# The first attention of a four-layer block: another order of its tiles, outputs kept by channel and divided with the help of DMAs and GpSimd, row maxima turned by VectorE

## The chip, the cores and the metric

The kernel runs on one core of one Trainium2 chip. The metric is the device time of one execution in microseconds (us); less is better. Each engine of the core works through a queue of its own: TensorE (PE; PEld is its loading of weights), VectorE (DVE), ScalarE (ACT), GpSimd (POOL) and SyncE (SP), which here does nothing but issue DMAs.

## What is computed

Four layers follow each other, each with a layer norm before it and a residual sum after it: an attention with 32 heads of 16 channels, a feed-forward layer with routed low-rank experts (FFN), an attention with 32 query heads of 128 channels, and the FFN again. The input has 1024 tokens of 512 channels, all in float32. Only the first attention is touched, and the projection after it:

```python
x = x + _L0_attn_a_ref(_layernorm(x, axis=-1), wq, wk, wv, wo)
# in it, with rotary embedding on xq and xk:
scores = jnp.einsum('bqhd,bkhd->bhqk', xq, xk) * scale
scores = jnp.where(causal[None, None], scores, NEG_INF)
probs = jax.nn.softmax(scores.astype(jnp.float32), axis=-1)
out = jnp.einsum('bhqk,bkhd->bqhd', probs, xv).reshape(B, T, C)
return out @ wo.T
```

## The kernel before

**Tiling.** The 32 heads are worked in 8 chunks (`NCA`) of 4 heads (`HC`). A head's 16 channels are padded to 32 partitions (`PADA`), so that the four heads of a chunk lie in the four quarters of `qT` and `kT` (128 partitions, chunk, 1024 tokens), and four score matmuls with 32 rows each can run beside each other in TensorE. Tokens come in 8 tiles of 128 (`NT`), queries also in two halves of 512 (`QC`; `qc` or `half` 0 is the low half).

**Two passes of scores.** The softmax needs the maximum of each query's row. So scores are made twice. The *row pass* (`row_scores`, L304) has queries on partitions; VectorE takes from it the negative maxima (`maxima`, L319) into `neg`. `with_maxima` (L341) turns `neg` so that queries lie along the free axis, and writes it into row 16 (`DA`) of every head in `qT`, where `kT` holds ones. The *column pass* (`col_scores`, L355) of the same chunk then has keys on partitions and yields scores with the maximum already subtracted; ScalarE takes the exponential (`exponentials`, L371), and `product` (L384) multiplies with the values. `v_p` has a 17th column of ones, so the products bring the sums of each row along, as row 16 of each head. A causal mask is added by one bf16 matmul per head on blocks on the diagonal (L380).

**Order.** `step(rc, cc, n)` (L440) does the n-th piece of the row pass of chunk `rc` and of the column pass of chunk `cc = rc - 1` together. It has two halves; in each, two heads make column scores and the other two make row scores, so that all four quarters of TensorE are in use. Then come maxima, exponentials, what is due from the list `later`, and half of the product of the step before last. The pieces of a chunk are listed by hand in `by_rows` and `by_cols` (L269 to L272): ten steps a chunk, of which two have 256 columns and the others 512; blocks on the diagonal occur in six of them. The row pass of chunk 0 runs in the prologue among the projections of q, k and v. The column pass begins with the low half; its maxima are written during the row pass's chunk, and those of the high half after step 0 of the column pass, which first uses them in step 3.

**Outputs.** When a half is complete, ScalarE copies it from PSUM (L407). One step later `normalize` (L410) transposes it on TensorE to tokens on partitions (L414), ScalarE copies it (L417), VectorE inverts the sums (L419), GpSimd multiplies in four pieces (L421) into `o`. After the last chunk `gather` (L1013) transposes `o` back to channels on partitions, tile by tile, and `out_projection` (L1019) multiplies with the output weights and adds to the residual: two tiles in `tail`, six among the first FFN.

**Queues and buffers.** All DMAs of this stage stand on SP's queue; the weights of the projection and the FFN are loaded on GpSimd's in the middle of it (`midway`). Score tiles share seven PSUM buffers (`ps_s`), outputs have one (`ps_o`). Waits between engines are set by the framework from what instructions read and write. An engine's order mostly follows the program, but the framework may lay an instruction later when it expects its inputs later.

Of the kernel before, what the change touches and what calls it, by code (L numbers as in the profile page):

```python
# [16 lines left out]
P = 128  # L17
T = 1024
# [46 lines left out]
class Block:  # L65
# [174 lines left out]
    def attend_a(self, ctx_pool, pt, work, ps_s, ps_o, qT, kT, v_p, project_qk, project_v, midway, tail):  # L240
        nc, tc = self.nc, self.tc
        HC = P // PADA
        with ExitStack() as ctx:
            cp = ctx.enter_context(tc.tile_pool(name="a_c", bufs=1))
            qk = ctx.enter_context(tc.tile_pool(name="a_qk", bufs=2))
            o_sb = []
# [22 lines left out]
            by_rows = [[(3, 0)], [(2, 0), (0, 0)], [(1, 0)], [(4, 0)], [(5, 0)], [(6, 0)], [(7, 0)]]  # L269
            by_rows += [[(7, 1)], [(6, 1), (4, 1)], [(5, 1)]]  # L270
            by_cols = [[(0, 0)], [(0, 1), (0, 3)], [(0, 2)], [(1, 0)], [(1, 1)], [(1, 2)], [(1, 3)]]
            by_cols += [[(1, 4)], [(1, 5), (1, 7)], [(1, 6)]]  # L272
            NP = len(by_rows)
# [21 lines left out]
            def row_pieces(n):  # L295
                return list(placed(by_rows[n], lambda i, kc: min(QC, (i + 1) * P - kc * QC)))

            def col_pieces(n):
                return list(placed(by_cols[n], lambda qc, b: min(QC, (qc + 1) * QC - b * P)))

            def on_diagonal(qc, b):
                return b * P >= qc * QC

            def row_scores(c, n, heads, made):  # L304

                for j in heads:
                    made[j] = ps_s.tile([P, QC], F32, tag="s", name=f"s{c}_{n}_{j}")
                for i, kc, at, end in row_pieces(n):
                    for j in heads:
                        nc.tensor.matmul(  # L310
                            made[j][:, at:end],
                            lhsT=qT[rows_of(j), c, i * P : (i + 1) * P],
                            rhs=kT[rows_of(j), c, kc * QC : kc * QC + end - at],
                            start=True,
                            stop=True,
                        )
                        yield

            def maxima(c, n, heads, made):  # L319

                for j in heads:
                    for i, kc, at, end in row_pieces(n):
# [18 lines left out]
            def with_maxima(c, half):  # L341

                rows = HC * NT // 2
                ps = ps_s.tile([P, QC], F32, tag="s", name=f"tp_m{c}{half}")[:rows, :P]
                nc.tensor.transpose(ps, neg(c, half).rearrange("p h i -> p (h i)"), self.ident)
                t = qk.tile([P, P], F32, tag="negT", name=f"negT{c}_{half}")[:rows, :]
                nc.scalar.copy(t, ps)
                for j in range(HC):
                    row = j * PADA + DA
                    nc.sync.dma_start(  # L350
                        qT[row : row + 1, c, half * QC : (half + 1) * QC].rearrange("o (i t) -> o i t", t=P),
                        t[j * NT // 2 : (j + 1) * NT // 2, :],
                    )

            def col_scores(c, n, heads, made):  # L355

                pieces = col_pieces(n)
                for j in heads:
                    made[j] = ps_s.tile([P, QC], F32, tag="s", name=f"sT{c}_{n}_{j}")
                for x, (qc, b, at, end) in enumerate(pieces):  # L360
                    for j in heads:
                        nc.tensor.matmul(  # L362
                            made[j][:, at:end],
                            lhsT=kT[rows_of(j), c, b * P : (b + 1) * P],
                            rhs=qT[rows_of(j), c, (qc + 1) * QC - (end - at) : (qc + 1) * QC],
                            start=x == 0,
                            stop=x == len(pieces) - 1 and not on_diagonal(qc, b),
                        )
                        yield

            def exponentials(n, heads, made, p):  # L371
                pieces = col_pieces(n)
                end = pieces[-1][-1]

                if on_diagonal(*pieces[0][:2]):
                    step = pieces[-1][2] // P or 1
                    mask = maskT.unsqueeze(1).to_broadcast([P, len(pieces), P])
                    for j in heads:
                        to = made[j].rearrange("p (a k) -> p a k", k=P)[:, : (len(pieces) - 1) * step + 1 : step, :]
                        nc.tensor.matmul(to, lhsT=identb, rhs=mask, start=False, stop=True)  # L380
                for j in heads:
                    nc.scalar.activation(p[:, j, :end], made[j][:, :end], AF.Exp)  # L382

            def product(c, n, p):  # L384

                first, last = n in (0, 3), n in (2, NP - 1)
                pieces = col_pieces(n)
                qc, middle = pieces[0][0], pieces[-1][-1] // 2
                if first:
                    outs[c, qc] = ps_o.tile([P, QC], F32, tag="o", name=f"oT{c}_{qc}")  # L390
                o = outs[c, qc]
                for lo, hi in ((0, middle), (middle, 2 * middle)):
                    for _, b, at, end in pieces:
                        x0, x1 = max(lo, at), min(hi, end)
                        for j in range(HC if x0 < x1 else 0):
                            nc.tensor.matmul(  # L396
                                o[rows_of(j), QC - end + x0 : QC - end + x1],
                                lhsT=v_cols(b, c * HC + j),
                                rhs=p[:, j, x0:x1],
                                start=first and x0 == 0,  # L400
                                stop=last and x1 == 2 * middle,
                            )
                    yield
                if not last:
                    return
                oT = work.tile([P, QC], F32, tag="w", name=f"oTs{c}_{qc}")
                nc.scalar.copy(oT, o)  # L407
                later.append(lambda: normalize(c, qc, oT))

            def normalize(c, qc, oT):  # L410
                if not o_sb:
                    o = ctx_pool.tile([P, NT, C], F32, tag="o", name="o")
                    o_sb.extend(o[:, i] for i in range(NT))
                ps = self.transpose4(ps_s, [oT[:, i * P : (i + 1) * P] for i in range(4)], f"o{c}{qc}", tag="s")  # L414
                pv = ps.rearrange("p a (h d) -> p a h d", d=PADA)
                os = qk.tile([P, 4, HC, DA + 1], F32, tag="os", name=f"os{c}_{qc}")
                nc.scalar.copy(os, pv[:, :, :, : DA + 1])  # L417
                rs = qk.tile([P, 4, HC], F32, tag="rs", name=f"rsa{c}_{qc}")
                nc.vector.reciprocal(rs, os[:, :, :, DA])  # L419
                for a in range(4):  # L420
                    nc.gpsimd.tensor_tensor(  # L421
                        o_sb[qc * 4 + a][:, c * HC * DA : (c + 1) * HC * DA].rearrange("p (h d) -> p h d", d=DA),
                        os[:, a, :, :DA],
                        rs[:, a, :].unsqueeze(2).to_broadcast([P, HC, DA]),
                        ALU.mult,
                    )
# [12 lines left out]

            def step(rc, cc, n):  # L440
# [3 lines left out]
                due = list(later)  # L444
                later.clear()
# [5 lines left out]
                for half in range(2 if both else 1):  # L451
# [11 lines left out]
                    if cc is not None:  # L463
                        exponentials(n, cols, madeT, p)
                    while due:
                        due.pop(0)()
                    next(turns, None)
                drain([turns])
                if rc is not None and n == 4:
                    later.append(lambda: with_maxima(rc, 0))  # L470
                if cc is not None and n == 0:
                    later.append(lambda: with_maxima(cc, 1))
# [9 lines left out]
            for _ in project_v:  # L482
                pass
            for c in range(NCA):
                if c == NCA // 2:
                    midway()
                for n in range(NP):
                    step(c + 1 if c + 1 < NCA else None, c, n)
            for item in pending:
                drain([product(*item)])  # L490
            tail(o_sb, ps_s, work, later)
        return o_sb
# [493 lines left out]
def hybrid_block_kernel(  # L986
# [26 lines left out]
    def gather(o, i, work, tp, wtag, tag):  # L1013
        ps = blk.transpose4(tp, [o[i][:, k * P : (k + 1) * P] for k in range(KC)], f"ao{i}", tag)
        oT = work.tile([P, KC * P], F32, tag=wtag, name=f"aoT{i}").rearrange("p (k t) -> p k t", t=P)
        nc.vector.tensor_copy(oT, ps)
        return oT

    def out_projection(i, oT, ps_m, tag):  # L1019
        pm = ps_m.tile([P, C], F32, tag=tag, name=f"pm_ao{i}")  # L1020
        for kc in range(KC):
            nc.tensor.matmul(pm, lhsT=oT[:, kc, :], rhs=wo[:, kc, :], start=(kc == 0), stop=(kc == KC - 1))  # L1022
        nc.vector.tensor_add(blk.x[i], blk.x[i], pm)

    def tail(o, ps, work, later):
        oTs = [gather(o, i, work, ps, "w", "s") for i in range(2)]
        out_projection(0, oTs[0], ps, "s")
        while later:
            later.pop(0)()
        out_projection(1, oTs[1], ps, "s")  # L1030
# [11 lines left out]
    def projected(work, tp, ps_m):  # L1042
        yield
        yield
        oT = gather(o, 2, work, tp, "oT", "tp")
        for i in range(2, NT):
            nxt = gather(o, i + 1, work, tp, "oT", "tp") if i + 1 < NT else None
            out_projection(i, oT, ps_m, "pm")
            oT = nxt
# [88 lines left out]
```

## Time and profile before

| | |
|---|---|
| median of 3 runs | 1655.16 us (1654.3 to 1655.9) |
| the profiled execution, its own time | 1654.29 us |
| its span, first to last instruction | 1652.2 us |
| prologue with projections (row pass of chunk 0 in it) | to 119.1 us |
| the eight column chunks | 119.1 to 401.3 us |
| first output projection begins | 402.75 us |
| DMAs `qT<-negT` of the first attention | 64, on SP |
| score matmuls, row and column (L310, L362) | 768 each in the trace, 169.6 and 160.5 us busy |

A row of an engine's group reads: line, engine, operation, written tile <- read tiles, shape, count; then busy time, mean of one in ns, and idle time before it with what ended it. A row of the timeline reads: start, length, engine, line, operation, tiles, count. A row of a single line gives durations as least/median/most in ns. A matmul in float32 appears as two records.

### The profile page before, as it was taken

How to read it: one execution, taken by the hardware profiler on the slowest of the kernel's cores; microseconds unless marked ns; L12 is line 12 of the kernel's file. 1: busy time of each engine (PE TensorE's matmuls, PEld its weight loads, DVE VectorE, ACT ScalarE, POOL GpSimd, SP SyncE). 2: the span in 40 equal slices, each digit the busy share in tenths (PEclk: the TensorE clock that was granted, in tenths of full speed). 3: DMA queues.
4: the chain of work that ended last, by engine and by line, in shares of the span. 5: the costliest groups of instructions: out<-in, count | busy, mean ns of one | idle time of the engine just before them, and what ended most of it. 6: DMA issues, size and time to landing. Idle time of an engine off the chain costs nothing.

```text
span 1652.2 us, 31905 instructions
## 1 busy us (share of the span) xinstructions
PE 1632.8 (99%) x12920; PEld 937.4 (57%) x12920; DVE 1100.7 (67%) x2832; ACT 555.2 (34%) x1230; POOL 351.6 (21%) x524
## 2 busy tenths in 40 slices
PE   9999999999999999999999999999999999999998
PEld 5544444444654657556655765655665576556654
DVE  4557777771553886776677677677667767777762
ACT  2325565555212333233233223223323322332230
POOL 3000000001311332223213222222322222222140
PEclk9999999999999999999999999999999999999999
DMA  5000000001003200200200120020020012000001
GB/s 198 1 1 2 3 2 2 2 2 40 1 27 88 65 1 27 65 27 26 65 27 7 51 60 2 27 65 26 27 65 26 16 45 64 1 27 27 2 1 51
DMA packets 60866, 52.03 MB, mean 31 GB/s; under 512 B 5744, under 2 KB 47472, under 8 KB 60720
## 3 DMA queue, kind: packets, MB, share of 16 engines
q1 hardware_dynamic: 59408, 46.06, 9.7%
q0 software_dynamic: 784, 2.90, 0.5%
q8 instruction: 101, 1.65, 0.4%
q10 hardware_dynamic: 528, 1.05, 0.2%
q14 instruction: 45, 0.37, 0.1%
HBM read 30.98 MB, written 2.10 MB: 20 GB/s over the span
## 4 chain that ended last, share of the span: by engine, by line
PE 95%; DVE 3%; ACT 1%; POOL 1%; issue 0%; ACTq 0%; DVEq 0%; POOLq 0%
PE s L798 15%; PE pq L752 13%; PE o L842 13%; PE wo L649 12%; PE sT L362 8%; PE kv L707 7%; PE oT L396 5%; PE pm_f L606 3%; PE or L842 3%; PE s L310 2%; PE pj_v L185 2%; PE pj_q L185 2%; PE pj_k L185 2%; PE sT L380 1%; PE pm_ao L1022 1%; PE st L778 1%
## 5 line engine op out<-in xcount | busy, mean ns | idle before, releaser
L807 ACT ACTIVATE p<-p,nm 128x1024 f32<-128x1024 f32 (+7 forms) x256 | 198.2, 774 | 405.3 <-DVE nm L805 363.6
L810 POOL TENSOR_SCALAR p<-p,rs 128x1024 f32<-128x1024 f32 (+7 forms) x256 | 190.9, 747 | 644.8 <-DVE rs L809 620.9
L798 PE MATMUL s<-kT,qT 128*128 128x512 f32 (+3 forms) x768 | 296.0, 493 | 1.9 <-DVE p L800 1.8
L825 DVE STREAM_TRANSPOSE pT<-p 128x640 f32<-128x640 f32 (+4 forms) x256 | 169.0, 670 | 128.6 <-PE o L842 84.5
L752 PE MATMUL pq<-xnTb,wq 128*128 128x512 f32 x512 | 243.0, 597 | 0.0
L649 PE MATMUL wo<-wo,oT 128*128 128x512 f32 x512 | 240.7, 593 | 1.8 <-DVE nm L805 1.8
L800 DVE SCALAR_TENSOR_TENSOR p<-s,rq,rel 128x512 f32<-128x512 f32 (+3 forms) x384 | 223.9, 601 | 24.6 <-PE s L798 23.4
L798 PEld LDWEIGHTS s<-kT,qT 128*128 128x128 f32 x768 | 140.8, 190 | 164.8 <-issue 117.7
L842 PEld LDWEIGHTS o<-pT,va 32*128 32x128 f32 x5248 | 210.7, 185 | 25.5 <-issue 17.9
L842 PE MATMUL o<-pT,va 32*128 32x256 f32 (+5 forms) x5248 | 220.0, 321 | 0.0
L382 ACT ACTIVATE p<-sT 128x512 f32<-128x512 f32 (+1 forms) x320 | 159.2, 554 | 107.1 <-PE sT L380 67.6
L804 DVE TENSOR_REDUCE nm<-p 128x1 f32<-128x1024 f32 (+7 forms) x256 | 188.7, 738 | 2.9
L310 PE MATMUL s<-kT,qT 32*128 32x512 f32 (+3 forms) x768 | 169.6, 524 | 0.0
L362 PE MATMUL sT<-qT,kT 32*128 32x512 f32 (+3 forms) x768 | 160.5, 524 | 0.0
L649 PEld LDWEIGHTS wo<-wo,oT 128*128 128x128 f32 x512 | 94.6, 190 | 89.0 <-issue 76.3
L752 PEld LDWEIGHTS pq<-xnTb,wq 128*128 128x128 f32 x512 | 92.4, 190 | 88.8 <-issue 79.7
L707 PE MATMUL kv<-wkv,xnTb 128*128 128x256 f32 x512 | 116.5, 380 | 0.8 <-DVE qT L762 0.5
L707 PEld LDWEIGHTS kv<-wkv,xnTb 128*128 128x128 f32 x512 | 96.3, 190 | 20.0 <-issue 4.0
L327 DVE TENSOR_REDUCE part<-s 128x1 f32<-128x512 f32 x128 | 82.0, 685 | 36.9 <-PE s L310 31.0
L362 PEld LDWEIGHTS sT<-qT,kT 32*128 32x128 f32 x768 | 61.5, 183 | 56.3 <-issue 37.8
L396 PE MATMUL oT<-p,v_p 128*32 128x256 f32 (+1 forms) x1408 | 93.0, 350 | 0.0
L421 POOL TENSOR_TENSOR o<-os,rsa 128x64 f32<-128x64 f32 x64 | 16.7, 293 | 338.5 <-DVE rsa L419 323.4
(154 smaller groups left out, 1623.2 us busy)
## 6 DMA issues: line engine op xcount, KB each, us to landing
va<-v SPq DMA_DIRECT2D x256, 64.0 KB
wq<-in_b_WqT_dram SPq DMA_DIRECT2D x8, 1024.0 KB
wo<-in_b_WoT_dram SPq DMA_DIRECT2D x8, 1024.0 KB
x<-in_x_dram SPq DMA_DIRECT2D x8, 256.0 KB
wkv<-in_b_WkT_dram SPq DMA_DIRECT2D x8, 256.0 KB
wkv<-in_b_WvT_dram SPq DMA_DIRECT2D x8, 256.0 KB
out_dram<-x SPq DMA_DIRECT2D x8, 256.0 KB
wq<-in_a_wqT_dram ACTq DMA_DIRECT2D x1, 1024.0 KB
```

The lines of the kernel that those rows point to most:

```text
L310: nc.tensor.matmul(made[j][:, at:end], lhsT=qT[rows_of(j), c, i * P : (i + 1) * P], rhs=kT[rows_of(j), c, kc * QC : kc * QC + end - at], s ...
L362: nc.tensor.matmul(made[j][:, at:end], lhsT=kT[rows_of(j), c, b * P : (b + 1) * P], rhs=qT[rows_of(j), c, (qc + 1) * QC - (end - at) : (qc ...
L396: nc.tensor.matmul(o[rows_of(j), QC - end + x0 : QC - end + x1], lhsT=v_cols(b, c * HC + j), rhs=p[:, j, x0:x1], start=first and x0 == 0, ...
L649: nc.tensor.matmul(ps, lhsT=oTs[g, h][:, t * P : (t + 1) * P], rhs=wo[:, h, :], start=(h == heads[0]), stop=(h == heads[-1]))
L707: nc.tensor.matmul(ps.rearrange("p a b -> p (a b)"), lhsT=xnT[:, kc, i * P : (i + 1) * P], rhs=wkv[:, kc].rearrange("p a b -> p (a b)"), s ...
L752: nc.tensor.matmul(ps, lhsT=wq[:, kc, hh * DB : (hh + 1) * DB], rhs=xnT[:, kc, cols], start=(kc == 0), stop=(kc == KC - 1))
L798: nc.tensor.matmul(s, lhsT=qT[:, i * P : (i + 1) * P], rhs=kT[:, lo:hi], start=True, stop=True)
L800: nc.vector.scalar_tensor_tensor(p[:, lo:hi], s, rq[:, i : i + 1], rel[:, at + lo : at + hi], ALU.mult, ALU.add)
L804: nc.vector.tensor_reduce(nm, p[:, :w], AX.X, ALU.max, negate=True)
L807: nc.scalar.activation(p[:, :w], p[:, :w], AF.Exp, bias=nm, scale=slope, accum_out=ss)
L810: nc.gpsimd.tensor_scalar(p[:, :w], p[:, :w], rs, 1.0, ALU.mult, ALU.mult)
L842: nc.tensor.matmul(cols(o[:, a], j), lhsT=vs[g][rows, j * NB + b, :], rhs=moving(j, rows, slice(b * B, (b + 1) * B)), start=(j == js[0] an ...
```

## The change

The order of the pieces is new: chunks 0 to 6 have nine column steps of 512 columns each (chunk 7 keeps ten). The four blocks on the diagonal of a half are gathered in one step of four 128-column pieces, so that only two steps of a chunk have a mask; what lies beside the diagonal comes in steps without one. The column pass of chunks 0 to 6 begins with the full blocks of the high half and ends with the low half; that of chunk 7 begins with the low half. The row passes have nine steps, in an order of their own (`up_rows` for chunks 0 and 7, `down_rows` for the others), and maxima are written once the last row piece of a half has been done.

`with_maxima` turns the maxima with a VectorE transpose of 32x32 blocks, with the 16 columns read twice to fill a block, where it used a TensorE transpose and a ScalarE copy. As each block of 32 queries then lies in partitions of its own, 16 DMAs write the four rows where there were 4.

`normalize` leaves the outputs with channels on partitions. Four DMAs spread the four rows of sums over 32 partitions each, four move the 16 channels of each head to their place in one tile `o` of 128 channels by 4 by 1024. Three half steps later `invert` takes the reciprocals on VectorE, and four DMAs bring them back to one row each and four more repeat each row over 16 partitions. Seven half steps after `normalize`, `multiply` does one GpSimd product over 64 partitions by 512. The output projection reads `o` as it is; `gather` is gone from it, in `tail` and in the first FFN.

The list `later` now holds a count of half steps with each entry, and `due` is called once a half (twice in steps that do only one pass).

```diff
-            by_rows = [[(3, 0)], [(2, 0), (0, 0)], [(1, 0)], [(4, 0)], [(5, 0)], [(6, 0)], [(7, 0)]]
-            by_rows += [[(7, 1)], [(6, 1), (4, 1)], [(5, 1)]]
-            by_cols = [[(0, 0)], [(0, 1), (0, 3)], [(0, 2)], [(1, 0)], [(1, 1)], [(1, 2)], [(1, 3)]]
-            by_cols += [[(1, 4)], [(1, 5), (1, 7)], [(1, 6)]]
-            NP = len(by_rows)
+            up_rows = [[(3, 0)], [(2, 0), (0, 0)], [(4, 0)], [(5, 0)], [(1, 0), (5, 1)], [(6, 0)], [(7, 0)], [(7, 1)]]
+            up_rows += [[(6, 1), (4, 1)]]
+            down_rows = [[(4, 0)], [(5, 0)], [(6, 0)], [(7, 0)], [(7, 1)], [(6, 1), (4, 1)], [(1, 0), (5, 1)], [(3, 0)]]
+            down_rows += [[(2, 0), (0, 0)]]
+            def diagonal(qc):
+                return [(qc, 4 * qc + a, a * P, (a + 1) * P) for a in range(4)]
+            def beside(qc, *blocks):
+                return [(qc, 4 * qc + a, (a + 1) * P, QC) for a in blocks]
+            full = [[(1, b, 0, QC)] for b in range(4)]
+            up_cols = [diagonal(0), beside(0, 0, 2), beside(0, 1), *full, diagonal(1), beside(1, 0, 2), beside(1, 1)]
+            down_cols = [*full, diagonal(1), beside(1, 0, 2), beside(1, 1) + beside(0, 1), diagonal(0), beside(0, 0, 2)]
+            def by_rows(c):
+                return up_rows if c in (0, NCA - 1) else down_rows
+            def by_cols(c):
+                return down_cols if c < NCA - 1 else up_cols
+            NP = len(down_rows)
...
             def with_maxima(c, half):
-                rows = HC * NT // 2
-                ps = ps_s.tile([P, QC], F32, tag="s", name=f"tp_m{c}{half}")[:rows, :P]
-                nc.tensor.transpose(ps, neg(c, half).rearrange("p h i -> p (h i)"), self.ident)
-                t = qk.tile([P, P], F32, tag="negT", name=f"negT{c}_{half}")[:rows, :]
-                nc.scalar.copy(t, ps)
+                t = qk.tile([P, B], F32, tag="negT", name=f"negT{c}_{half}")
+                twice = neg(c, half).rearrange("p h i -> p (h i)").unsqueeze(1).to_broadcast([P, 2, B // 2])
+                nc.vector.transpose(t.rearrange("p (a m) -> p a m", a=2), twice)
                 for j in range(HC):
                     row = j * PADA + DA
-                    nc.sync.dma_start(
-                        qT[row : row + 1, c, half * QC : (half + 1) * QC].rearrange("o (i t) -> o i t", t=P),
-                        t[j * NT // 2 : (j + 1) * NT // 2, :],
-                    )
+                    to = qT[row : row + 1, c, half * QC : (half + 1) * QC].rearrange("o (i a t) -> o a i t", a=P // B, t=B)
+                    for a in range(P // B):
+                        m = a * B + j * NT // 2
+                        nc.sync.dma_start(to[:, a], t[m : m + NT // 2, :])
...
-                            rhs=qT[rows_of(j), c, (qc + 1) * QC - (end - at) : (qc + 1) * QC],
+                            rhs=qT[rows_of(j), c, qc * QC + x0 : qc * QC + x1],
                             start=x == 0,
-                            stop=x == len(pieces) - 1 and not on_diagonal(qc, b),
+                            stop=x == len(pieces) - 1 and not masked,
...
-                if on_diagonal(*pieces[0][:2]):
-                    step = pieces[-1][2] // P or 1
+                if pieces[0][:4] in diagonal(pieces[0][0]):
                     mask = maskT.unsqueeze(1).to_broadcast([P, len(pieces), P])
                     for j in heads:
-                        to = made[j].rearrange("p (a k) -> p a k", k=P)[:, : (len(pieces) - 1) * step + 1 : step, :]
+                        to = made[j].rearrange("p (a k) -> p a k", k=P)
                         nc.tensor.matmul(to, lhsT=identb, rhs=mask, start=False, stop=True)
                 for j in heads:
                     nc.scalar.activation(p[:, j, :end], made[j][:, :end], AF.Exp)
...
+                        last = p1 == end and b == [x[1] for y in steps for x in y if x[0] == qc][-1] and all(
+                            x[0] != qc for y in steps[n + 1 :] for x in y
+                        )
...
+                        if last:
+                            oT = qk.tile([P, QC], F32, tag="oT", name=f"oTs{c}_{qc}")
+                            nc.scalar.copy(oT, o)
+                            normalize(c, qc, oT)
                     yield
-                if not last:
-                    return
-                oT = work.tile([P, QC], F32, tag="w", name=f"oTs{c}_{qc}")
-                nc.scalar.copy(oT, o)
-                later.append(lambda: normalize(c, qc, oT))
             def normalize(c, qc, oT):
-                if not o_sb:
-                    o = ctx_pool.tile([P, NT, C], F32, tag="o", name="o")
-                    o_sb.extend(o[:, i] for i in range(NT))
-                ps = self.transpose4(ps_s, [oT[:, i * P : (i + 1) * P] for i in range(4)], f"o{c}{qc}", tag="s")
-                pv = ps.rearrange("p a (h d) -> p a h d", d=PADA)
-                os = qk.tile([P, 4, HC, DA + 1], F32, tag="os", name=f"os{c}_{qc}")
-                nc.scalar.copy(os, pv[:, :, :, : DA + 1])
-                rs = qk.tile([P, 4, HC], F32, tag="rs", name=f"rsa{c}_{qc}")
-                nc.vector.reciprocal(rs, os[:, :, :, DA])
-                for a in range(4):
-                    nc.gpsimd.tensor_tensor(
-                        o_sb[qc * 4 + a][:, c * HC * DA : (c + 1) * HC * DA].rearrange("p (h d) -> p h d", d=DA),
-                        os[:, a, :, :DA],
-                        rs[:, a, :].unsqueeze(2).to_broadcast([P, HC, DA]),
-                        ALU.mult,
-                    )
+                if not outs_sb:
+                    outs_sb.append(ctx_pool.tile([P, KC, T], F32, tag="o", name="o"))
+                at = c % 2 * HC * DA
+                to = outs_sb[0][at : at + HC * DA, c // 2, qc * QC : (qc + 1) * QC]
+                sums = qk.tile([P, QC // B], F32, tag="sums", name=f"sums{c}_{qc}")
+                over = qk.tile([P, QC], F32, tag="over", name=f"over{c}_{qc}")
+                row = P // 2 - at
+                for j in range(HC):
+                    r = j * PADA + DA
+                    nc.sync.dma_start(sums[j * B : (j + 1) * B, :], oT[r : r + 1, :].rearrange("o (x e) -> o x e", x=B))
+                for j in range(HC):
+                    nc.sync.dma_start(to[j * DA : (j + 1) * DA, :], oT[j * PADA : j * PADA + DA, :])
+                def invert():
+                    nc.vector.reciprocal(sums, sums)
+                    for j in range(HC):
+                        nc.sync.dma_start(
+                            over[row + j : row + j + 1, :].rearrange("o (x e) -> o x e", x=B), sums[j * B : (j + 1) * B, :]
+                        )
+                    for j in range(HC):
+                        nc.sync.dma_start(
+                            over[at + j * DA : at + (j + 1) * DA, :],
+                            over[row + j : row + j + 1, :].unsqueeze(1).to_broadcast([1, DA, QC]),
+                        )
+                def multiply():
+                    nc.gpsimd.tensor_tensor(to, to, over[at : at + HC * DA, :], ALU.mult)
+                later.append([2, invert])
+                later.append([6, multiply])
...
+            def due():
+                for x in list(later):
+                    x[0] -= 1
+                    if x[0] < 0:
+                        later.remove(x)
+                        x[1]()
...
-                    while due:
-                        due.pop(0)()
+                        exponentials(cc, n, cols, madeT, p)
+                    due()
+                    if not both:
+                        due()
                     next(turns, None)
-                if rc is not None and n == 4:
-                    later.append(lambda: with_maxima(rc, 0))
-                if cc is not None and n == 0:
-                    later.append(lambda: with_maxima(cc, 1))
+                if rc is not None:
+                    for half in range(2):
+                        if n == max(m for m, y in enumerate(by_rows(rc)) for x in y if x[0] // 4 == half):
+                            later.append([0, lambda half=half: with_maxima(rc, half)])
...
-                pass
+                due()
-                for n in range(NP):
+                for n in range(len(by_cols(c))):
                     step(c + 1 if c + 1 < NCA else None, c, n)
             for item in pending:
+                due()
                 drain([product(*item)])
-            tail(o_sb, ps_s, work, later)
-        return o_sb
+            tail(outs_sb[0], ps_s, later)
...
-    def gather(o, i, work, tp, wtag, tag):
-        ps = blk.transpose4(tp, [o[i][:, k * P : (k + 1) * P] for k in range(KC)], f"ao{i}", tag)
-        oT = work.tile([P, KC * P], F32, tag=wtag, name=f"aoT{i}").rearrange("p (k t) -> p k t", t=P)
-        nc.vector.tensor_copy(oT, ps)
-        return oT
-    def out_projection(i, oT, ps_m, tag):
+    def out_projection(oT, i, ps_m, tag):
         pm = ps_m.tile([P, C], F32, tag=tag, name=f"pm_ao{i}")
         for kc in range(KC):
-            nc.tensor.matmul(pm, lhsT=oT[:, kc, :], rhs=wo[:, kc, :], start=(kc == 0), stop=(kc == KC - 1))
+            nc.tensor.matmul(pm, lhsT=oT[:, kc, i * P : (i + 1) * P], rhs=wo[:, kc, :], start=(kc == 0), stop=(kc == KC - 1))
         nc.vector.tensor_add(blk.x[i], blk.x[i], pm)
-    def tail(o, ps, work, later):
-        oTs = [gather(o, i, work, ps, "w", "s") for i in range(2)]
-        out_projection(0, oTs[0], ps, "s")
+    def tail(oT, ps, later):
+        out_projection(oT, 0, ps, "s")
         while later:
-            later.pop(0)()
-        out_projection(1, oTs[1], ps, "s")
+            later.pop(0)[1]()
+        out_projection(oT, 1, ps, "s")
...
-        oT = gather(o, 2, work, tp, "oT", "tp")
         for i in range(2, NT):
-            nxt = gather(o, i + 1, work, tp, "oT", "tp") if i + 1 < NT else None
-            out_projection(i, oT, ps_m, "pm")
-            oT = nxt
+            out_projection(o, i, ps_m, "pm")
             yield
```

## Prediction, made before the changed kernel was run

> **What bounds the kernel now.** I read the page first (parts 1 and 4), then the first attention by stretches, its instruction groups with shapes kept apart, the timeline of TensorE over one chunk, and at last the SP queue: its rows by line, its timeline and its waits.
>
> ```profile
> PE 1632.8 (99%) x12920; PEld 937.4 (57%) x12920; DVE 1100.7 (67%) x2832; ACT 555.2 (34%) x1230; POOL 351.6 (21%) x524
> PE 95%; DVE 3%; ACT 1%; POOL 1%; issue 0%; ACTq 0%; DVEq 0%; POOLq 0%
> ```
>
> TensorE is busy throughout and carries 95% of the chain that ended last. So work taken from it is worth its time, and any wait that is put before it costs its time.
>
> ```profile
> 191.80:228.10 36.30, 36.02 (x406) 15.75 (x402) 25.88 (x82) 21.77 (x46) 2.09 (x8) 1.00 0.01 2
> ```
>
> This is the stretch view over about one chunk in the middle of the first attention: length, then busy time of PE, PEld, DVE, ACT, POOL, then the granted clock. PE 36.0 of 36.3, DVE 25.9, ACT 21.8, clock 1.00. The same step (first score matmul of step 1) starts at 194.51 and 231.12 us in the timeline: 36.6 us a chunk. Chunk 0 has no products in its first two steps and takes 35.3; it starts at 119.1, chunk 7 at 374.0, and the output projection at 402.75.
>
> ```profile
> 202.20 0.69 PE L362 MATMUL sT<-qT,kT 32*128 32x512 f32 x1
> 203.27 0.64 PE L396 MATMUL oT<-p,v_p 128*32 128x256 f32 x8
> 216.44 0.69 PE L362 MATMUL sT<-qT,kT 32*128 32x512 f32 x1
> 199.62 0.66 PE L99 MATMUL tp_o<-ident,oTs 128*128 128x128 f32 x4 [0.28 <-ACT oTs L407]
> ```
>
> Between 202.20 and 216.44 lie four full steps (3 to 6) and 0.8 us of transposes: 3.36 us a full step. A group of output transposes costs 0.58 to the next start and 0.28 of waiting.
>
> ```profile
> L350 SPq DMA_DIRECT2D qT<-negT x64: 572/573/748, 97.7 to 381.8; - x64
> 379.82 2.57 SPq L350 DMA_DIRECT2D qT<-negT  x4
> 544.79 21.74 SPq L723 DMA_DIRECT2D va<-v  x32
> L1075 SPq DMA_DIRECT2D out_dram<-x x8: 332/333/360, 1615.5 to 1648.9; - x8
> SPq L669 <- DMA qT<-negT: 1.0, 1, 1.0
> ```
>
> These rows decide the case. Issuing one small DMA from SBUF to SBUF holds SP's queue for 573 ns; four in a row take 2.57 us (0.643 each), 32 of another shape 21.74 (0.679 each). The last line is SP itself waiting for such a transfer: 1.0 us from the end of its issue until it has landed. Today a chunk has 8 of these, and nobody waits for them.
>
> **What is taken from TensorE.** Per chunk: the transposes of outputs, 2 x 0.86 = 1.7; the two of maxima, 2 x 0.2 = 0.4; one step fewer, and the mask in two steps instead of six. I add up the rest anew: nine full steps x 3.36 = 30.2. A mask of two heads took 0.21 us at 128 columns and 0.32 at 256, so 0.53 at 512; twice in each of two diagonal steps: 2.1. Sum 32.4 against 36.6. The four 128-wide pieces of a diagonal step keep pace with the 512-wide rows beside them: in the timeline 128-wide passes follow each other at 0.11 us. DVE's 25.9 and ACT's 21.8 still fit under 32.4. In the first FFN six groups of transposes go, about 0.5 each with their waits: 3.1. If nothing stood against it: chunk 0 from 118.5 (the prologue loses a 0.64 us row step), 31.1 for it, 6 x 32.4: chunk 7 at 344 instead of 374.0, 1.2 less within it, 3.1 less later. That is 34 us less.
>
> Small additions beside other work: 16 reciprocals at 0.25 (row 128x16) replace as many; 16 GpSimd products of 512 columns at 1.27 (row x<-x,w_small) replace 64 at 0.29, 20.3 for 18.8 us on an engine that is 6% busy here; 16 VectorE transposes 128x32, not in the trace, lie between 0.1 and the 0.67 mean of the 128x640 transposes; I take 0.25, as for 128x16. ACT loses the copies.
>
> **What is put on SP.** `with_maxima` now issues 4 heads x 4 blocks = 16 DMAs instead of 4, `normalize` 4 + 4, `invert` 4 + 4. Per chunk 2 x 32 = 64, in all 512 against 64. No row shows the new shapes. From below: 0.33 to 0.4, the plain 128-partition store; from above 0.68, the va row. I take 0.643, that of the nearest row: the same source, destination and kind. Then SP needs 64 x 0.643 = 41.2 us a chunk. That is more than TensorE's 32.4, and more than today's 36.6.
>
> Here a rule of the Trainium skill speaks against me: "DMA: Bandwidth & Descriptors", section "Issuing engines are not separate DMA queues", holds the sequencer's time for starting a DMA to be usually small beside the DMA itself. The row says 573 ns to issue and 1.0 us to land for 2 KB. By the rule the change gives 1621; by the row the queue is the bound.
>
> **Who waits.** Chunks 0 to 6 now begin with the full blocks of queries 512 to 1023, whose maxima are complete only after row step 6 of the chunk before. So their 16 DMAs (call them M1) have steps 7 and 8, 4.4 + 3.4 = 7.8 us, to be in place. They need 0.9 for VectorE to end, 0.25 transpose, 16 x 0.643 = 10.3 and 1.0 landing, 12.5 in all. Even on an empty queue TensorE waits 4.7. And the queue isn't empty: between one M1 and the next stand 8 of `normalize`, the other 16 maxima, 8 of `invert`, 8 and 8 again, 30.9 us. M1 would be ready 24.6 + 1.2 us after the chunk began; SP is free after 29.9. So a chunk takes 41.2.
>
> In time (us): the prologue's last row step ends at 111.2, maxima of four heads 2.8, transpose, 16 DMAs from 114.3, landed 125.6: chunk 0 starts there instead of 119.1. Its M1 starts at 150.1 and lands at 161.4, chunk 1. Then five times 41.2: chunk 6 at 367.4. Chunk 7 begins with the low half, whose maxima (due after row step 4) go out behind the 48 others: 366.4 + 64 x 0.643 + 1.0 = 408.6. Its step 3 needs the high half: 8 + 16 more, landed 424.0. Seven steps remain, which take 19.8 today, 18.8 then: 442.8. Meanwhile 40 DMAs (25.7) bring the last division of the low half to 449.7, product 1.3: the projection starts at 451.0 instead of 402.75. That is +48.2; less 3.1 in the FFN: +45. The last division of the high half (16 more DMAs, about 461) is needed by tile 4, some 20 us after the projection begins, and is hidden. The loads for the second attention go out behind them and have till about 530.
>
> The profiled execution took 1654.29 us, 2.1 beside its span of 1652.2. 1654.3 + 45 = 1699; it lies 0.9 below the median of 1655.16, so 1700.
>
> The clock: it is 1.00 everywhere today, PE never pausing. "TensorE: Matmul & The Clock Gate", Part 1, says the array falls to half clock after an idle window of about 3.4 us and needs as long to recover. By the trace a stall costs its length; by the rule 1.7 us more, an estimate. With 41.2 a chunk there are 4.1 us (29.9 - 25.8) in which that hides. Where the queue isn't the bound it adds up.
>
> **Rivals.**
> 1. *Only the maxima are late* (chance 0.20). If the 32 plainer DMAs cost about 0.4, SP needs 20.6 + 12.8 = 33.4 and is not the bound; M1's latency is: 24.6 + 12.5 = 37.1 a chunk. Chunk 7 then starts at 379, its step 3 at 395, the projection at 414.5: +9, 1664; with eight cold starts at 1.7 it is 1677. For it: stores of 333 ns. Against it: every SBUF to SBUF row is 572 or more.
> 2. *VectorE waits as well* (0.22). `invert` follows `normalize` by three half steps, but its row sums stand behind the queue: those of the low half land 23 us after a chunk's start, while program order puts the reciprocal in step 3, at 10 us. Maxima queue behind it; the seven PSUM buffers fill by about 13, and TensorE stands till 23. M1 then starts at 36 and lands at 47: 6 more in each of five chunks, 1730. Against it: the order of instructions may be laid out later than the program has it, as a reciprocal that isn't ready need not stand first.
> 3. *The other side: issue is cheap or hidden* (0.07), 1621 as worked out. It decides where the mean price falls below 36.6 / 64 = 0.57 for the queue and, for M1, 16 prices + 2.2 below 7.8 + 4.2, 0.61; with the prologue's loss, about 0.5 for all shapes. The new maxima DMA moves 512 B instead of 2 KB, which would have to count; but 573 (2 KB) and 585 to 599 (64 KB) say that size doesn't.
>
> **How the numbers follow.** Likeliest, with 0.49: SP's queue is the bound, 1700. Near no change 0.02. Faster by over 0.2% (about what a measurement of this kernel can tell from no change) 0.07, within 0.02, slower 0.91. The range reaches to rival 1 without its cold starts' full size (1665) and to rival 2 with 0.66 a DMA (64 x 0.017 x 6 = 6.5 on 1730, so 1738); it leaves out the faster cases and some 0.1 at both ends.
>
> **What would show it.** Right: SP's DMAs nearly without gaps from about 114 to 460, 573 to 600 ns each, 512 of them; TensorE idle some 8 us at each chunk's start, released by the qT DMAs; a period near 41; the clock below 1 in those slices. Rival 1: gaps on SP and a period of 37. Rival 2: VectorE's reciprocal released by DMA into sums, several us each. Wrong: a period near 32, or issue rows of 0.3 us.

## The result, and the profile after

The changed kernel takes 1780.34 us (median of 4 runs, 1776.02 to 1780.59) against 1655.15: ratio 1.075, 95% interval 1.0732 to 1.0769. It is 125 us slower; the prediction had slower, by 45. The profiled execution took 1780.37 us with a span of 1778.2. The page, part 1, the slices of PE and of its granted clock, and part 4:

```profile
PE 1667.5 (94%) x13208; PEld 963.6 (54%) x13208; DVE 1095.8 (62%) x2840; ACT 546.4 (31%) x1170; POOL 354.3 (20%) x476
...
PE   9989677787779999999999999999999999999998
...
PEclk9989787888879999999999999999999999999999
...
PE 85%; SPq 7%; DMA 3%; DVE 3%; POOL 1%; issue 1%; ACT 1%; DVEq 0%; POOLq 0%; ACTq 0%
```

The slices of PE before:

```profile
PE   9999999999999999999999999999999999999998
```

A slice is 44.5 us. PE was full everywhere; now slices 5 to 12 (most of the first attention) have holes, and the clock is at 0.7 to 0.8 in the same slices. SP and DMA have come into the chain of waits, yet SP's 7% alone does not make it the bound. The timeline of SP over one chunk shows more (M1, as in the prediction, are the 16 DMAs of the high half's maxima, without which the next chunk can't begin; here those at 207.58 and 261.59):

```profile
207.58 10.13 SPq L366 DMA_DIRECT2D qT<-negT  x16
217.81 2.46 SPq L441 DMA_DIRECT2D sums<-oTs  x4
220.31 2.48 SPq L443 DMA_DIRECT2D o<-oTs  x4
222.91 10.08 SPq L366 DMA_DIRECT2D qT<-negT  x16
233.09 2.42 SPq L448 DMA_DIRECT2D over<-sums  x4
235.61 2.44 SPq L452 DMA_DIRECT2D over<-over  x4
238.10 2.48 SPq L441 DMA_DIRECT2D sums<-oTs  x4
240.63 2.48 SPq L443 DMA_DIRECT2D o<-oTs  x4
243.23 2.67 SPq L448 DMA_DIRECT2D over<-sums  x4
246.01 2.44 SPq L452 DMA_DIRECT2D over<-over  x4
261.59 10.13 SPq L366 DMA_DIRECT2D qT<-negT  x16
```

The 64 DMAs of a chunk stand in the predicted order and near the predicted price (16 in 10.13 us, 0.63 each against 0.643), 207.58 to 248.45 without a gap: 40.9 us. Then SP has nothing to do for 13.1 us, until the next chunk's first maxima are turned. So SP is full for 41 us of a chunk of 54.0 and waits for somebody else. Who that is, the waits view of 207 to 316 us (two chunks) and VectorE's timeline tell; in brackets stands the idle time before an instruction and what ended it:

```profile
DVE sums L446 <- DMA sums<-oTs: 36.9, 4, 11.6
...
PE sT L376 <- DVE part L342: 19.1, 2, 9.7
...
PE sT L376 <- DMA qT<-negT: 6.8, 4, 2.0
```

```profile
221.54 0.25 DVE L446 RECIPROCAL sums<-sums 128x16 f32<-128x16 f32 x1 [6.46 <-DMA sums<-oTs]
...
230.97 0.69 DVE L342 TENSOR_REDUCE part<-s 128x1 f32<-128x512 f32 x1 [0.35 <-PE sT L376]
242.84 0.25 DVE L446 RECIPROCAL sums<-sums 128x16 f32<-128x16 f32 x1 [11.18 <-DMA sums<-oTs]
243.01 2.41 DVE L342 TENSOR_REDUCE part<-s 128x1 f32<-128x512 f32 x4
...
261.30 0.21 DVE L360 STREAM_TRANSPOSE negT<-neg 128x32 f32<-128x32 f32 x1
```

VectorE stands 11.18 us at the reciprocal of the low half, whose row sums were issued only at 238.10, behind 48 other DMAs of the chunk. The reductions (L342, which take the maxima) queued behind it come out at 243.01 in one block of four: they were ready and could not pass. The transpose that starts the next M1 comes at 261.30, and that is what SP waits for. TensorE, in its own timeline:

```profile
216.33 0.66 PE L376 MATMUL sT<-qT,kT 32*128 32x512 f32 x1 [2.02 <-DMA qT<-negT]
...
218.85 1.19 PE L376 MATMUL sT<-qT,kT 32*128 32x512 f32 x1 [1.40 <-DMA qT<-negT]
...
224.64 0.69 PE L376 MATMUL sT<-qT,kT 32*128 32x512 f32 x1
...
243.69 1.22 PE L376 MATMUL sT<-qT,kT 32*128 32x512 f32 x1 [9.30 <-DVE part L342]
...
251.68 0.59 PE L325 MATMUL s<-kT,qT 32*128 32x512 f32 x1
```

Two stalls a chunk: 2.02 + 1.40 for M1, and 9.30 because no score buffer came free while VectorE stood. After each, a 512-column pass lasts 1.19 or 1.22 instead of 0.66, until 224.64 (5.8 us) and until 251.68 (8.0 us). The stretch view has the granted clock at 0.50 there (third figure from the end):

```profile
217.50:224.30 6.80, 5.45 (x36) 2.03 (x40) 1.89 (x5) 1.52 (x3) 0.00 (x0) 0.50 0.10 21
238.00:251.60 13.60, 7.91 (x52) 3.72 (x56) 4.71 (x10) 1.68 (x3) 1.26 (x1) 0.50 0.54 29
```

The same sequences at full clock come to about 3.2 and 4.3 (an estimate from passes at full clock), so the restarts cost about 2.6 and 3.7.

### The profile page after: what moved, and what is told of

Read it like the earlier page. It is cut to its first block, busy times and chain, and to the rows that moved or that the text cites. A ratio compares the mean times of both kernels' runs of the same rounds, so it can differ in the third digit from the quotient of the medians.

```text
span 1778.2 us, 32990 instructions
## 1 busy us (share of the span) xinstructions
PE 1667.5 (94%) x13208; PEld 963.6 (54%) x13208; DVE 1095.8 (62%) x2840; ACT 546.4 (31%) x1170; POOL 354.3 (20%) x476
## 3 DMA queue, kind: packets, MB, share of 16 engines
q1 hardware_dynamic: 71184, 50.54, 13.1%
## 4 chain that ended last, share of the span: by engine, by line
PE 85%; SPq 7%; DMA 3%; DVE 3%; POOL 1%; issue 1%; ACT 1%; DVEq 0%; POOLq 0%; ACTq 0%
PE s L843 14%; PE pq L797 12%; PE o L887 12%; PE wo L694 12%; PE sT L376 7%; PE kv L752 6%; SPq L366 4%; PE oT L415 4%; PE pm_f L651 3%; PE or L887 2%; PE s L325 2%; PE pj_q L185 2%; PE pj_k L185 2%; PE pj_v L185 1%; SPq L448 1%; PE st L823 1%
## 5 line engine op out<-in xcount | busy, mean ns | idle before, releaser
L376 PE MATMUL sT<-qT,kT 32*128 32x128 f32 (+3 forms) x1152 | 204.0, 450 | 85.9 <-DVE part L342 58.0
L325 PE MATMUL s<-kT,qT 32*128 32x512 f32 (+3 forms) x768 | 203.6, 580 | 0.0
L376 PEld LDWEIGHTS sT<-qT,kT 32*128 32x128 f32 x1152 | 96.5, 207 | 158.5 <-DVE part L342 69.8
L458 POOL TENSOR_TENSOR o<-o,over 64x512 f32<-64x512 f32 x16 | 20.2, 1265 | 459.0 <-DMA over<-over 415.6
L342 DVE TENSOR_REDUCE part<-s 128x1 f32<-128x512 f32 x128 | 81.2, 680 | 36.7 <-PE s L325 31.0
L415 PE MATMUL oT<-p,v_p 128*32 128x128 f32 (+1 forms) x1552 | 99.7, 363 | 1.5 <-ACT oTs L424 1.5
```

The source lines that it names most:

```text
L325: nc.tensor.matmul(made[j][:, at:end], lhsT=qT[rows_of(j), c, i * P : (i + 1) * P], rhs=kT[rows_of(j), c, kc * QC : kc * QC + end - at], s ...
L376: nc.tensor.matmul(made[j][:, at:end], lhsT=kT[rows_of(j), c, b * P : (b + 1) * P], rhs=qT[rows_of(j), c, qc * QC + x0 : qc * QC + x1], st ...
L415: nc.tensor.matmul(o[rows_of(j), x0 + p0 - at : x0 + p1 - at], lhsT=v_cols(b, c * HC + j), rhs=p[:, j, p0:p1], start=first, stop=last,)
```

## The experiments

The theory that this profile suggests (A): VectorE's in-order wait for the sums is the bound, SP's queue only makes it long. The rival: SP's queue (or the lateness of the maxima) is the bound, and VectorE's wait lies in its shadow. All ratios are to the kernel before, with the 95% interval; its medians beside these runs were 1654.55 to 1654.84.

**e1: take the reciprocal from VectorE.** GpSimd does it as a power.

```diff
-                    nc.vector.reciprocal(sums, sums)
+                    nc.gpsimd.tensor_tensor(sums, sums, minus, ALU.pow)   # minus: a tile of -1.0
```

> The changed kernel with one thing other: the reciprocal of the row sums is a GpSimd power of -1 instead of a VectorE reciprocal, so that the wait for the sums' DMAs no longer stands among the maxima. Theory A (VectorE, waiting in its own order for sums that are behind SP's queue, is what the prediction left out, together with the slow clock after it): the stall of some 9 us and the slow stretch behind it go from each chunk, the period falls from 54 to 41 to 44 us (SP's 64 DMAs), and the kernel takes 1700 to 1720. Theory B (the queue and the late maxima are the whole cause, VectorE only waits where TensorE would have waited anyway): within 15 us of 1780.

1734.59 us, 1.0479 (1.0464 to 1.0495): 46 us come back, fewer than A had said. In SP's and GpSimd's timelines:

```profile
241.65 10.12 SPq L368 DMA_DIRECT2D qT<-negT  x16
...
275.64 2.49 SPq L445 DMA_DIRECT2D o<-oTs  x4
281.37 2.42 SPq L450 DMA_DIRECT2D over<-sums  x4
...
287.17 10.13 SPq L368 DMA_DIRECT2D qT<-negT  x16
```

```profile
277.22 1.27 POOL L460 TENSOR_TENSOR o<-o,over 64x512 f32<-64x512 f32 x1 [17.38 <-DMA over<-over]
278.46 2.89 POOL L448 TENSOR_TENSOR sums<-sums,minus 128x16 f32<-128x16 f32 x1
```

The chunk is 45.5 us from M1 to M1: SP's 41, a hole of 3.2 (278.13 to 281.37) and short waits. In the hole SP waits for GpSimd's power, 2.89 us for 16 columns, which itself stood behind a product. With VectorE free, SP is the bound, as predicted; before that it was not. The hole, which A's figure had not counted, comes once a chunk, some 20 us in all; the run is 15 above A's range.

**e2: turn the maxima as before, keep the rest.** TensorE transpose, ScalarE copy and 4 DMAs in `with_maxima`, as on the minus lines of the change.

> The changed kernel with the maxima turned as before: TensorE transpose, ScalarE copy, 4 DMAs of 512 queries' rows instead of 16; order and outputs are the changed ones. SP has 40 DMAs a chunk, 25 us at 0.63. Theory A: the sums stand behind at most 4 other DMAs, VectorE waits 0 to 2 us, no stall at the chunk's start: 1622 to 1645, faster than before. A rival C, that the outputs by way of DMAs cost by themselves (sums that land after the reciprocal's place even on an empty queue): 1660 to 1720, with VectorE's reciprocal waiting several us a chunk.

1694.53 us, 1.0237 (1.0221 to 1.0252): A's figure fails, rival C holds. SP now has 40 DMAs a chunk instead of 64, but VectorE still waits twice a chunk (its timeline, one chunk):

```profile
239.96 0.25 DVE L448 RECIPROCAL sums<-sums 128x16 f32<-128x16 f32 x1 [2.96 <-DMA sums<-oTs]
...
254.60 0.25 DVE L448 RECIPROCAL sums<-sums 128x16 f32<-128x16 f32 x1 [4.81 <-DMA sums<-oTs]
```

The sums of the first wait were issued at 235.48, after SP had stood idle for 2.0 us, so the wait does not need a full queue: issue and landing alone take longer than the place of the reciprocal in VectorE's order allows. TensorE, which has no slack, loses it and its clock with it:

```profile
240.82 1.12 PE L325 MATMUL s<-kT,qT 32*128 32x512 f32 x2 [1.66 <-DVE part L342]
...
242.75 1.22 PE L378 MATMUL sT<-qT,kT 32*128 32x512 f32 x1
...
255.45 1.00 PE L378 MATMUL sT<-qT,kT 32*128 32x512 f32 x1 [2.87 <-DVE part L342]
```

It is 44.1 us from M1 to M1, of which TensorE stands 4.5.

**e3: the new order of the pieces alone** (maxima and outputs as before), run twice, and **e4: the new maxima alone** in the kernel before.

> Only the new order of the pieces (nine steps, the diagonal by itself); maxima and outputs as before. By the sum of the prediction: a step's overhead 0.7 and masks 0.85 a chunk, so 8 to 14 us less than before, 1641 to 1648. If the shorter way from the last maxima to the chunk's start (7.8 us) is too short even for 4 DMAs: near 1655 or above.

> The kernel before with only its maxima turned by VectorE and written by 16 DMAs. Its high half has the steps 0 to 2 of its chunk, some 10 us, and needs 12.5. Theory A and the sum of the prediction: a stall of 2 to 4 us a chunk with no slow clock or little of it, against 0.4 saved: 1660 to 1690. If the 16 DMAs by themselves were harmless: 1650 to 1656.

e3: 1639.82 us, 0.9908 (0.9891 to 0.9924), 15 us faster than before. e4: 1660.93, 1.0036 (1.0023 to 1.0049), at the low end of its range, but not by the stall of 2 to 4 us a chunk that was expected. In the old order the high half's maxima have the steps 0 to 2 of their chunk to arrive, and that nearly always is enough: TensorE waits for them in two places, 1.7 us in all, the longer one in the last chunk, where no row pass fills the steps:

```profile
387.10 2.04 PE L360 MATMUL sT<-qT,kT 32*128 32x512 f32 x2 [1.44 <-DMA qT<-negT]
```

The clock is 0.50 from 386.9 to 393.8, and the projection starts 6.3 us later than before: the loss lies in the last chunk, most of it in this one stall and its clock. The 16 DMAs hurt where the order needs them early.

**e8: order and new maxima, outputs as before.**

> The changed kernel with the outputs as before (transposed on TensorE, divided by tokens, gathered); order and maxima are the changed ones. SP has 32 DMAs a chunk, all maxima, and nothing else. By the prediction's sum the high half's 16 need 12.5 us where 7.8 are left, a stall of 4.7 at the start of each of chunks 1 to 6 on an empty queue, 7 in the prologue, and with the clock's recovery some 2.5 more each: 1680 to 1695. If only a full queue made them late: 1640 to 1650.

1692.94 us, 1.0227 (1.0212 to 1.0242). TensorE's timeline at a chunk's start:

```profile
203.87 0.66 PE L376 MATMUL sT<-qT,kT 32*128 32x512 f32 x1 [1.89 <-DMA qT<-negT]
...
206.39 1.19 PE L376 MATMUL sT<-qT,kT 32*128 32x512 f32 x1 [1.40 <-DMA qT<-negT]
```

On a queue with room (32 DMAs a chunk) M1 is late by 1.89 + 1.40, as in the full change, and the clock is lost with it. These late maxima are worth 53 us over e3.

**e5: e1 and e2 together.**

> The changed kernel with the maxima turned as before (4 DMAs) and the reciprocal on GpSimd: no VectorE wait for DMAs and 40 DMAs a chunk on SP. Theory A (the 54.7 us between this order with the new outputs and with the old ones are VectorE's waits and the slow clock behind them): the period falls from 44 to 32.5 to 34 us and the kernel takes 1620 to 1640, at or below the order alone (1640). Rival C (the outputs' DMAs cost otherwise, by their landing or by what they do to other transfers): stays above 1660.

1650.27 us, 0.9972 (0.9961 to 0.9984). The chunks run without stalls, but at the end of the attention the projection waits about 13 us for the last outputs and their division (12.7 is the longest such wait), which the expected figure had left out.

**e6: e2 with the reciprocal late.** It is held in program order and called after 6 half steps instead of 2, the product after 12 instead of 6. In chunk 7 the low half's product then comes behind the first tile's projection, so that this projection reads 64 channels not yet divided; the work is the same.

> The kernel with the maxima back, its VectorE reciprocal kept in program order and put off to the seventh half step after the outputs' copy (product at the thirteenth), so that it stands behind maxima that are ready and its sums have landed. Nothing is moved to another engine. Theory A: as the reciprocal on GpSimd, 1620 to 1640. If the reciprocal still waits: 1660 to 1695.

1637.45 us, 0.9895 (0.988 to 0.991). **e9** does it without that: chunk 7 keeps the old delays.

```diff
-                    nc.vector.reciprocal(sums, sums)
+                    tc.keep_in_program_order(nc.vector.reciprocal(sums, sums))
...
-                later.append([2, invert])
-                later.append([6, multiply])
+                later.append([6 if c < NCA - 1 else 2, invert])
+                later.append([12 if c < NCA - 1 else 6, multiply])
```

> The changed kernel with the maxima turned as before (4 DMAs), and the reciprocal held in VectorE's program order and called later: after 6 half steps instead of 2, the product after 12 instead of 6; for chunk 7 the old delays stay, so everything is divided before the projection. Theory A (VectorE's in-order wait for the sums is what the outputs by DMA cost; with the sums landed before the reciprocal's turn nothing is left of it in the chunks): no idle time of VectorE before the reciprocals of chunks 0 to 6, a period of 32 to 34 us, and in the end a wait of 5 to 13 us for the last division: 1638 to 1648 us. Rival B (the broadcast DMAs slow the maxima's landing, so that TensorE waits whatever VectorE does): above 1655.

1643.54 us, 0.993 (0.9917 to 0.9942): 51 us below e2, by a later place for a quarter-microsecond instruction and for the DMAs and the product that hang on it. That the instruction matters and not the place of the DMAs, e5 says as well: it left the delays as they were, and its chunks have no stalls either. The stretch view over four chunks (columns as in the prediction):

```profile
188.70:323.07 134.37, 134.37 (x1773) 68.75 (x1771) 101.89 (x332) 82.97 (x160) 10.19 (x8) 1.00 0.28 19
```

TensorE is never idle, clock 1.00, 33.6 us a chunk. The wait for GpSimd's last product, 8.9 us, stays.

**e10: the same late reciprocal in the full change,** with all 64 DMAs a chunk. **e11: the reciprocal only held in program order,** delays as they were.

> The changed kernel with all its DMAs (16 for each turn of maxima), only the reciprocal held in VectorE's program order and called after 6 half steps (the product after 12; chunk 7 as it was). Theory A (VectorE's wait is taken away, SP's 64 issues of 0.64 us are then the bound, with no GpSimd power in their chain): a period of 41 to 42.5 us, SP without gaps, 10 to 25 us below the kernel with GpSimd's reciprocal (1735): 1705 to 1725, near the prediction's 1700. Rival B (a queue-bound chunk costs TensorE its clock after each stall, and the chain of the low half's division is what fills the hole): a period of 44 to 45 as with GpSimd's reciprocal, 1730 to 1745. Rival C (the wait of VectorE only moves to another place): above 1760.

> The changed kernel with the reciprocal held in VectorE's program order, delays unchanged. Theory A: the framework had laid the low half's reciprocal about a step earlier than the program has it; in its program place it still waits for the sums behind SP's queue, but some 3 us less, so TensorE's stall of 9.3 us a chunk falls to about 6: 1745 to 1770. Rival B: the place in the order counts for nothing, as the maxima behind it fill the PSUM buffers all the same: 1775 to 1785.

e10: 1720.56 us, 1.0393 (1.0379 to 1.0407). SP over one chunk:

```profile
240.29 10.11 SPq L366 DMA_DIRECT2D qT<-negT  x16
...
285.50 10.13 SPq L366 DMA_DIRECT2D qT<-negT  x16
```

M1 starts at 196.69, 240.29, 285.50, 329.32 and 372.66: 44.0 on average, 41 of issue and the rest SP's own waits, mostly for `over<-sums` to land before it is spread (6.9 us over four chunks, up to 1.8 each). This is the kernel I had predicted: the queue is the bound, and it costs 66 us, of which rival B had the period and A the sum. e11: 1760.21, 1.0637 (1.0623 to 1.0652): the framework had laid the reciprocals three and four reductions *earlier* than the program has them (a step has four). In its own place it still waits:

```profile
239.92 0.25 DVE L446 RECIPROCAL sums<-sums 128x16 f32<-128x16 f32 x1 [8.57 <-DMA sums<-oTs]
```

8.57 instead of 11.18, and 20 us less in all.

**e7: e1 with the DMAs of the outputs on GpSimd's queue.**

> The kernel with the reciprocal on GpSimd (1735) with the 32 DMAs a chunk of the outputs issued from GpSimd's queue instead of SP's; SP keeps the 32 of the maxima, 20 us a chunk. If SP's queue is what bounds that kernel (period 45), the period falls to what the late maxima allow, 37 to 40 with the slow clock after their stall, and the kernel takes 1680 to 1705. If it is not, or if GpSimd's own issuing takes as long: 1725 or more.

1700.23 us, 1.027 (1.0255 to 1.0286): 34 us below e1. Where VectorE is out of the way, relieving SP helps, but M1's own lateness stays, as TensorE's timeline at a chunk's start shows:

```profile
201.35 0.66 PE L378 MATMUL sT<-qT,kT 32*128 32x512 f32 x1 [1.87 <-DMA qT<-negT]
...
203.96 1.19 PE L378 MATMUL sT<-qT,kT 32*128 32x512 f32 x1 [1.49 <-DMA qT<-negT]
```

**e12: e3 once more, beside e9.**

> The new order of the pieces alone (old turn of the maxima, old outputs) once more, beside the late reciprocal on the same chip, to tell which is faster: 1638 to 1642 us.

1639.38 us, 0.9902 (0.9887 to 0.9918). It beats the kernel before and the changed one, and e9 (the intervals just touch: 0.9918 and 0.9917), by 4 us in the medians. The useful part of the change is its order.

## Why the prediction was wrong

- **TensorE's work: right, slightly small.** I summed 32.4 us a chunk; e9 without stalls has 33.6, of which 0.4 are transposes of maxima that the change does away with. Mis-sized was what the outputs' transposes free: 1.0 us a chunk (34.6 in e3, 33.6 in e9), not 1.7. For the order alone my figures leave 34 − 8 x 2.1 − 3.1 = 14 us of gain; e3 measured 15.
- **SP's price: right.** 573 ns, 0.63 in a row, 64 in 40.9 us. The page of the Trainium skill that I weighed ("DMA: Bandwidth & Descriptors", "Issuing engines are not separate DMA queues") calls starting a DMA usually small beside the DMA; here a small one took 0.57 us to issue and about 1.3 from then to land, and e7 shows that a second issuing queue is worth 34 us.
- **M1 late by 4.7 us on an empty queue: right in kind.** It was 3.3 in e8 and 3.4 in the full change. Chunk 0 started at 124.6 (125.6 predicted), and the first M1 was turned at 152.8 (issue from 150.1 predicted).
- **"SP's queue is the bound, 41.2 us a chunk": this step failed.** M1 was to start at 356 for chunk 6 and started at 423.39, 13 us later per chunk, which is SP's idle time of 13.1. Rival 2 had the mechanism: VectorE waits for sums that stand behind the queue, the buffers fill, TensorE stands. I gave it 0.22, because I counted on the framework to lay a reciprocal that isn't ready *later*. It laid it earlier, and e11 prices that at 20 us. Rival 2 itself was too small: it had 47 us a chunk and 1730, the chip 54.0 and 1780; it had left out the clock, below. With VectorE's wait gone (e10) 1720.56 remain against 1700, and this part of the miss is in the queue-bound chunk itself: SP's waits for its own `over<-sums` and for other engines, some 2.8 us a chunk, had no term in the 41.2, and M1 for chunk 6 starts at 372.66 instead of 356.
- **The clock: mis-sized, and wrongly hidden.** I took 1.7 us a stall from "TensorE: Matmul & The Clock Gate", Part 1, as an estimate, and let it vanish in 4.1 us of slack of a queue-bound chunk. It came to about 2.6 and 3.7, as full clock returned 5.8 and 8.0 us after work had resumed. Nor did it take the idle window of about 3.4 us: stands of 1.66 (e2) and 2.02 us were enough. What stays of that figure is a beat: the granted clock was at 0.50 for 3.41 and 6.8 us in e2, for 6.8 in e4, e8 and e11 and for 6.8 and 13.6 in the full change, one, two or four times 3.41, so a stall's price depended on where it fell on the beat and not on its length alone. Since SP was not the bound there was no slack, and the lost time delayed the next maxima: +6.3 a chunk, half of the 13.

The chunk in sum: 33.2 of work at full clock, 3.4 for M1, 2.6, 9.3 for VectorE, 3.7: 52.2 of 54.0. The 1.8 left over fit what the stalls did to the half steps they fell into. A half step's two pairs of heads run beside each other and take 1.07 us together (224.64 to 225.71); each stall came between the two, and the first pair alone took 1.13 (from 216.33 and from 233.26): 2.2 for both, an estimate. Along one path of the runs the 125 us are, rounded, −15 for the order (e3), +55 for outputs by way of DMA (e2 over e3), +86 for the maxima on top (full change over e2). Taken the other way round the maxima cost 53 (e8 over e3) and the outputs 87. Each alone costs about 54, and another 33 comes with both on one queue. With the reciprocal on GpSimd, both on two queues cost 60 over e3 (e7), about the sum of each alone (53 in e8, 10 in e5), and on one queue 95 (e1). Shown is: VectorE's wait is worth 51 us without the 16 DMAs (e2 to e9) and 60 with them (full change to e10). Only argued is that the queue makes the 33 with VectorE's reciprocal too, and how they divide between longer waits and colder clock.

## What to carry to other kernels

A result that comes back by DMA must not be read early by an engine that others depend on: in an in-order queue a 0.25 us instruction stood 11 us and stopped everything behind it. Cost such an instruction from the landing time of its input and its *actual* place in the queue, not from where the program or a favourable scheduler would put it; hold it in place, late, if there is slack. And where the bound engine has no slack, add its slow clock to each stall, even to one of 2 us, and more than once if there are several a chunk.

## What was not expected of the hardware

- The granted clock in the full change switched at 217.5, 224.3, 238.0 and 251.6 us, all on one beat of 3.41 us.
- GpSimd's power of 128x16 took 2.90 us, more than twice its product of 64x512 (1.27).
- A VectorE transpose of 128x32 took 0.21 us, less than the 0.25 assumed.
- In e9 the DMA engines are busy 28% of the time with these small transfers (1% in the stretch of before) while the chunks lose nothing by it. They can lengthen a landing: in e2 the high half's sums were there 1.27 us after their last issue (239.96 after 238.69), those of the low half, behind four `over<-over`, 3.10 us (254.60 after 251.50), with the DMA engines busy at 0.79 from 249.06 to 252. No run separates this part of VectorE's wait from the rest.
